# fp8 rounding in single pieces between key tiles, K and Q of the first layer evicted by ScalarE, and constants loaded in two lots

## The chip, the cores and the metric

The kernel runs on one core of a Trainium2 chip. The metric is the device time of one execution in microseconds; a time given for the kernel is the median of several runs. Profiled executions give, beside their own time, every instruction with its engine, start and duration. The engines are TensorE (PE for its matmuls, PEld for its weight loads), VectorE (DVE), ScalarE (ACT), GpSimd (POOL) and SyncE (SP), which issues most of the DMA transfers.

## What is computed

Two layers over a sequence of 4096 tokens of 256 features, in float32. Cut to what matters here:

```python
xn = layernorm(x)
# layer 0: strided sparse attention (16 heads of 16) and an fp8 product, both added to x
q, k, v = split(xn @ c_attn_w + c_attn_b)      # keys: every 8th position of all, and the own block of 128
x_q = (bf16(xn) / s_in).astype(float8_e4m3fn)
k_q = (kernel / s_k).astype(float8_e4m3fn)
y   = bf16(x_q @ k_q * (s_in * s_k)) + bias
x   = x + attention(q, k, v) @ c_proj_w + c_proj_b + y
# layer 1: rotary causal attention, a second causal attention with normalised heads, and four experts
x   = x + attention1(layernorm(x)) + experts(...)
```

The kernel does not use an fp8 type for the rounding. It rounds in float32 arithmetic: the quotient by the scale with its correction (four operations), the rounding to the spacing of fp8 by adding and subtracting a large power of two times the exponent (two on VectorE and two on GpSimd), and what lies beyond the range of fp8 (four).

## The kernel before

The sequence is worked in eight chunks of 512 positions (`NCH`, `CW`), four tiles of 128 each, and the heads in four groups of four. A *unit* is one attention kind `a` (0: sparse, 1 and 2: the causal ones), one group and one chunk of queries. A unit of the sparse attention is 1.25 key chunks long: four key tiles of strided keys and one of the own blocks. For every key tile TensorE makes scores (`st_a`), ScalarE their exponentials (`pt_a`), and TensorE multiplies them by the values (`po_a`). The maxima of a unit that comes two key chunks later are made beside this: TensorE makes products into a ring of three PSUM banks (`pms_a` strided, `pml_a` own, `pm_a` causal) and VectorE reduces them to `mx_a`. A unit ends with ScalarE's copy of `po_a` to `oc_a`.

**The order of work** is written out by hand. `Schedule` (from line 67) takes pieces with a key, and hands them out in order of the keys. One unit of the key is one key chunk of attention; key 0 is the first score tile, and what prepares the first two chunks' worth of keys has negative keys. The five engines are wrapped in `InOrder` (line 39), which makes each engine issue in just the order in which the pieces were handed out. So whatever an engine waits for, everything of its own that was handed out later waits too. As every instruction goes through the wrapper, almost all of them have line 53 in the profile, and they are told apart by their tiles.

Scores and maxima of a key tile have keys at 0.06 and 0.185 (and every quarter further), values at 0.2. `spread(start, end, todo)` places side work between key tiles: item `i` of `n` gets the key

```python
key = start + (end - start) * i / len(todo)
put(0.25 * np.floor((key - 0.2) / 0.25) + 0.212 + 1e-4 * i, *item, delay=0.9e-4)
```

so it is moved back to the slot ahead of a key tile, and all items of one slot are handed out one after the other. `block` places lists side by side in one short stretch, without this rounding to slots; chunks 4 to 7 are prepared in blocks beside the experts of an earlier chunk.

**Preparation of a chunk** (`prepare0`): `fetch` loads x and weight columns (tags `x`, `w0`); `normalised` makes the layernorm, statistics on VectorE (`bn`, `mv`, `ve`), the power and the scaling on GpSimd (`rs`, `x`); `turn` transposes on TensorE and ScalarE copies to `xt` (tag `xt0`; `ht` for the strided positions). Then K and Q products (`pk`, `pq`): VectorE evicts them with the bias (`sk`, `sq`, tag `r2`), ScalarE makes the rounded high part and GpSimd the remainder (`hl_k`, `hl_q`), and SP stores both to DRAM. V products go the same way to `v_d`. The chunk's `rounds` are, for each of the two halves of the features, a bf16 copy of `xt` by ScalarE (`xb`) and the three pieces of `quantise` (tiles `qz_x`, and `qa_x` and `qb_x` of tag `r2`, two buffers). The result `xq` goes into the products `ys` (`py`, `y`, stored to `y_d`), which need the rounded fp8 kernel `kq`; `kernel_pieces` loads that (`kern`, into the buffer `xb`) and rounds it by the same function (`qz_k`, `qa_k`, `qb_k`).

`prepare0(NCH)` is the preparation of the strided positions, K and V only. The first chunk's and the strided positions' preparation are handed out ahead of everything. `ys` of chunk 0 carries the first load of six expert weights (`weights.fetch`), after its two products.

**The constants** are loaded by ScalarE's DMA queue, one instruction each, before ScalarE's first copy.

Of the kernel before, what the change touches and what calls it, by code (L numbers as in the profile page):

```python
# [9 lines left out]
F32 = mybir.dt.float32  # L10
# [10 lines left out]
E = 256  # L21
# [88 lines left out]
def tile_two_layers(ctx: ExitStack, tc, d, out):  # L110
# [52 lines left out]
    with ExitStack() as at:  # L163
# [35 lines left out]
        for i in range(2):  # L199
# [6 lines left out]
        nc.vector.tensor_scalar(qkw[:, 0:1], qkw[:, 0:1], 0.25, None, ALU.mult)  # L206
        bqk = load("bqk", [P, 4], F32, c1)
        nc.vector.tensor_scalar(bqk[:, 0:2], bqk[:, 0:2], 0.25, None, ALU.mult)
        bv = load("bv", [P, E], F32, c1, d["bv"].partition_broadcast(P))
        bproj = load("bproj", [P, E], F32, c1, d["bproj"].partition_broadcast(P))  # L210
        fbias = load("fbias", [P, E], BF16, c1, d["fbias"].partition_broadcast(P))
        wp = [
            load(n, [P, 2, w], F32, c1, d[n].rearrange("(c p) n -> p c n", p=P))
            for n, w in (("wp0", E), ("wp1", E), ("wp2", EO))
        ]
        nw2 = load("nw2", [P, 2], F32, c1)
        gatew = load("gate", [P, 2, 4], F32, c1, d["gate"].rearrange("(c p) n -> p c n", p=P))
        tri = load("tri", [P, 2, 16], F32, c1, d["tri"].partition_broadcast(P))
        vst, vst_no = [], [0]
        for i in range(2):  # L220
            t = c1.tile([P, 2, H, D + 1], F32, name=f"vst{i}")
# [18 lines left out]
        nc.vector.tensor_tensor(sprod, scales[:, 0:1], scales[:, 1:2], ALU.mult)  # L240
        kq = c1.tile([P, 2, E], BF16, name="kq")

        def quantise(todo, q, v, k, name):


            sc = slice(k, k + 1)
            s = {}

            def quotient():
                zt = work.tile([P, CW], BF16, tag="qz", name=f"qz_{name}")  # L250
                a, b = (work.tile([P, CW], F32, tag="r2", name=f"{i}_{name}", bufs=2) for i in ("qa", "qb"))
                s.update(a=a, b=b)
                v_ = v()
                dve.tensor_scalar(zt, v_, rscale[:, sc], None, ALU.mult)
                dve.scalar_tensor_tensor(a, zt, nshi[:, sc], v_, ALU.mult, ALU.add)
                dve.scalar_tensor_tensor(b, zt, nslo[:, sc], a, ALU.mult, ALU.add)
                dve.scalar_tensor_tensor(a, b, rscale[:, sc], zt, ALU.mult, ALU.add)

            def rounded():

                a, b = s["a"], s["b"]
                dve.tensor_scalar(b.bitcast(I32), a.bitcast(I32), 0x7F800000, None, ALU.bitwise_and)
                dve.tensor_scalar(b, b, 2.0**-6, 1.5 * 2.0**20, ALU.max, ALU.mult)
                pool.tensor_tensor(a, a, b, ALU.add)
                pool.tensor_tensor(a, a, b, ALU.subtract)

            def bounded():

                a, b = s["a"], s["b"]
                dve.tensor_scalar(b.bitcast(I32), a.bitcast(I32), 0x7FFFFFFF, None, ALU.bitwise_and)  # L270
                dve.tensor_scalar(b, b, 448.0, 3e38, ALU.is_gt, ALU.mult)
                dve.tensor_scalar(b, b, 3e38, None, ALU.mult)
                dve.scalar_tensor_tensor(q(), b, 0.0, a, ALU.mult, ALU.add)

            todo += [(f, None, None) for f in (quotient, rounded, bounded)]

        def turn(todo, src, evict, name):

# [57 lines left out]
            split(s, hl)  # L336
            stored(dst, hl, half, col, what)

        def normalised(todo, x, nm):

            s = {}

            def moments():
                st = small.tile([P, TPC, 6], F32, tag="bn", name="bn" + nm)
                s["mv"] = small.tile([P, TPC, 2], F32, tag="mv", name="mv" + nm)
                for t in range(TPC):
                    dve.bn_stats(st[:, t, :], x()[:, t, :])
                    dve.bn_aggr(s["mv"][:, t, :], st[:, t, :])
                ve = small.tile([P, TPC], F32, tag="ve", name="ve" + nm)
                dve.tensor_scalar(ve, s["mv"][:, :, 1], LN_EPS, None, ALU.add)  # L350
                s["rs"] = small.tile([P, TPC], F32, tag="rs", name="rs" + nm)
                pool.tensor_tensor(s["rs"], ve, mhalf[:, :TPC], ALU.pow)

            def applied():
                for t in range(TPC):
                    pool.tensor_scalar(
                        x()[:, t, :], x()[:, t, :], s["mv"][:, t, 0:1], s["rs"][:, t : t + 1],
                        ALU.subtract, ALU.mult,
                    )

            todo += [(moments, None, None), (applied, None, None)]
# [50 lines left out]
        def prepare0(ch, w=None):  # L412
# [16 lines left out]
                w.fetch(2)  # L429

            act_piece(fetches, fetch)
            normalised(head, lambda: s["x"], nm)

            def kept(f, pt):
                if f == 0:
                    s["xt"] = work.tile([P, 2, CW], F32, tag="ht" if strided else "xt0", name="xt" + nm)
                act.copy(s["xt"][:, f, :], pt)

            turn(turns, lambda: s["x"], kept, "pt" + nm)
# [1 line left out]
            def rounded(f):  # L441
                def rounded16():
                    if f == 0:
                        s["xq"] = work.tile([P, 2, CW], BF16, tag="xq", name="xq" + nm)
                    s["xb"] = work.tile([P, CW], BF16, tag="xb", name=f"xb{f}{nm}")
                    act.copy(s["xb"], s["xt"][:, f, :])

                act_piece(rounds, rounded16)
                quantise(rounds, lambda: s["xq"][:, f, :], lambda: s["xb"], 0, f"x{f}{nm}")

            for i, (what, dst) in enumerate((("k", k_d[0]), ("q", q_d[0]))):
                if strided and what == "q":
                    continue
                for half in range(2):
                    z = {}

                    def fill(z=z, i=i, half=half, what=what):
                        feature_product(z, w[i], s["xt"], half, f"p{what}{half}{nm}")

                    def drain(z=z, half=half, what=what):  # L460
                        z["s"] = work.tile([P, CW], F32, tag="r2", name=f"s{what}{half}{nm}", bufs=2)
                        if what == "q":
                            dve.tensor_scalar(z["s"], z["p"], 0.25, bqk[:, half : half + 1], ALU.mult, ALU.add)
                        else:
                            dve.tensor_scalar(z["s"], z["p"], bqk[:, 2 + half : 3 + half], None, ALU.add)

                    def store(z=z, half=half, what=what, dst=dst):
                        split_stored(z["s"], dst, half, col, what, f"{what}{half}{nm}")

                    todo = halves_[i if own else half]  # L470
                    todo.append((fill, "bank", drain))
                    act_piece(todo, store)
# [813 lines left out]
        def kernel_pieces():  # L1286
            todo, s = [], {}

            def fetch():
                s["k"] = work.tile([P, CW], BF16, tag="xb", name="kern")  # L1290
                sp.dma_start(
                    s["k"].rearrange("p (c n) -> p c n", c=2), d["fkernel"].rearrange("(c p) n -> p c n", p=P)
                )

            todo.append((fetch, None, None))
            quantise(todo, lambda: kq.rearrange("p c n -> p (c n)"), lambda: s["k"], 1, "k")
            return todo

        place, plan = [0.0], []
# [27 lines left out]
        def spread(start, end, todo):  # L1327

            for i, item in enumerate(todo):
                key = start + (end - start) * i / len(todo)  # L1330
                put(0.25 * np.floor((key - 0.2) / 0.25) + 0.212 + 1e-4 * i, *item, delay=0.9e-4)

        w = Columns("ew", Stream.AHEAD, [("w0", 1), ("w0", 0), ("w0", 2)], "first")
        fetches, head, turns, (first, second), vs = prepare0(NCH, w)
        fetches0, head0, turns0, (first0, second0), vs0, rounds, ys = prepare0(0, w)
        block(-2000.0, (fetches + fetches0 + head + head0 + turns + turns0 + first + first0, 0.0, 1.0))
        block(-1.72, (vs + vs0 + second + second0, 0.0, 1.0), size=0.8)
        spread(0.0, 0.6, rounds)
# [197 lines left out]
```

## Time and profile before

| | us |
|---|---|
| median of 3 runs | 5078.9 (5078.31 to 5078.94) |
| the profiled execution | 5070.28 |
| its span, first to last instruction | 5068.5 |

| engine | busy us | share of the span | instructions |
|---|---|---|---|
| PE | 4862.3 | 96% | 34528 |
| PEld | 2548.9 | 50% | 34528 |
| DVE | 3711.4 | 73% | 8425 |
| ACT | 3274.0 | 65% | 6927 |
| POOL | 664.3 | 13% | 781 |

Times within the execution are counted from the start of the span. The page cuts the span into 40 equal slices and gives each engine's busy share in tenths; PEclk is the clock that the chip granted TensorE in the slice, in tenths of the full one. A view of stretches gives the same for any stretch in us. In a timeline a row is an instruction or several alike: start, duration, engine, operation, what it writes and reads, and in brackets how long its engine was idle before and what ended that. Matmul ends are modelled, so a busy PE is not PE at its peak.

### The profile page before, as it was taken

To read this page: it belongs to the slowest core of one execution; us is meant where nothing else is said; L and a number is where in the kernel's file an instruction comes from. 1 tells how busy PE (TensorE), PEld (TensorE's weight loads), DVE (VectorE), ACT (ScalarE), POOL (GpSimd) and SP (SyncE) were. 2 spreads that over 40 slices of the span, in tenths; PEclk is the share of its full clock that TensorE was granted. 3 is DMA by queue.
4 is the path that set the end of the run, shared out by engine and by line. 5 is a ranking of instruction groups with operands and counts; after the bars stand their busy time and mean duration, and the time that the engine had idled before them with its cause. 6 is when DMAs were issued, how large, how long until landed. Compare 5 with 4: busy or idle time off the path is not lost. (4 is left out here: it accounts for less than half of the span.)

```text
span 5068.5 us, 94907 instructions
## 1 busy us (share of the span) xinstructions
PE 4862.3 (96%) x34528; PEld 2548.9 (50%) x34528; DVE 3711.4 (73%) x8425; ACT 3274.0 (65%) x6927; POOL 664.3 (13%) x781
## 2 busy tenths in 40 slices
PE   6788799999999999999999999999999999999999
PEld 3445455555655564545545455544445544444445
DVE  5666685787588848897588885798984898989701
ACT  2456484676467747776477774677774777777752
POOL 3233313112100130102201002001002000000000
PEclk8889899999999999999999999999999999999999
DMA  5555545544534463434634334434333433333222
GB/s 195 179 171 187 191 162 180 179 157 157 190 134 148 141 207 128 143 130 143 202 121 152 124 126 137 164 112 145 121 126 118 161 121 128 115 108 131 94 79 75
DMA packets 480300, 732.85 MB, mean 145 GB/s; under 512 B 84053, under 2 KB 185941, under 8 KB 479833
## 3 DMA queue, kind: packets, MB, share of 16 engines
q1 hardware_dynamic: 475424, 724.33, 42.8%
q8 instruction: 273, 4.47, 0.4%
q10 hardware_dynamic: 4408, 2.46, 0.2%
q14 instruction: 195, 1.59, 0.1%
HBM read 582.71 MB, written 143.95 MB: 143 GB/s over the span
## 5 line engine op out<-in xcount | busy, mean ns | idle before, releaser
L53 ACT ACTIVATE pt_a<-st_a 128x512 f32<-128x512 f32 (+3 forms) x5248 | 2595.7, 571 | 935.1 <-PE st_a L53 862.1
L53 DVE TENSOR_REDUCE mx_a<-pm_a 128x1 f32<-128x512 f32 x3584 | 2220.8, 681 | 281.8 <-PE pm_a L53 170.8
L53 PE MATMUL pm_a<-km_a,q_a 64*128 64x512 f32 (+3 forms) x4608 | 1825.1, 435 | 59.4 <-DVE mx_a L53 49.4
L53 PE MATMUL st_a<-q_a,ke_a 64*128 64x512 f32 (+3 forms) x5632 | 1792.9, 403 | 19.8 <-ACT pt_a L53 15.6
L53 PE MATMUL st_a<-rows,pick_r 64*128 64x512 f32 (+3 forms) x5248 | 1766.6, 402 | 0.0
L53 PEld LDWEIGHTS st_a<-q_a,ke_a 64*128 64x128 f32 x5632 | 913.5, 188 | 1036.8 <-ACT pt_a L53 888.0
L53 PE MATMUL po_a<-pt_a,v 128*32 128x512 f32 (+3 forms) x11264 | 1334.6, 552 | 0.0
L53 PEld LDWEIGHTS pm_a<-km_a,q_a 64*128 64x128 f32 x4608 | 846.6, 186 | 437.8 <-DVE mx_a L53 381.7
L53 PEld LDWEIGHTS st_a<-rows,pick_r 64*128 64x128 f32 x5248 | 953.5, 187 | 61.0 <-issue 2.0
L53 DVE CUSTOM_DVE_ANT_0 pm_a<-pm_a,never_sb 128x512 f32<-128x512 f32 (+3 forms) x1024 | 479.0, 514 | 125.6 <-PE st_a L53 68.2
L53 DVE CUSTOM_DVE_ANT_0 pms_a<-pms_a,hidden_sb 128x512 f32<-128x512 f32 x512 | 339.1, 718 | 59.5 <-PE pms_a L53 46.7
L53 PEld LDWEIGHTS po_a<-pt_a,v 128*32 128x32 f32 x11264 | 228.7, 108 | 304.9 <-issue 266.8
L53 POOL CAST pad<-nm_a 128x16 fp32r<-128x16 f32 x96 | 19.6, 205 | 2280.0 <-DVE nm_a L53 2280.0
L53 PE MATMUL pms_a<-km_a,q_a 64*128 64x512 f32 x512 | 227.3, 508 | 77.8 <-DVE mx_a L53 61.3
L53 ACT CAST rows<-tu_a 8x128 fp32r<-8x128 f32 x768 | 227.1, 296 | 106.5 <-DVE tu_a L53 94.0
L53 DVE SCALAR_TENSOR_TENSOR acc_m<-pe_m,g_wt_m,acc_m 128x192 f32<-128x192 f32 x128 | 53.2, 417 | 314.7 <-PE pe_m L53 309.9
L53 PE MATMUL st_a<-mcol_sb,identb_sb 64*128 64x128 bf16 x2048 | 253.7, 225 | 0.0
L53 DVE DVE_READ_ACCUMULATOR2_ANT mx_a<- 128x1 f32 x1536 | 215.9, 141 | 0.0
L53 PEld LDWEIGHTS pms_a<-km_a,q_a 64*128 64x128 f32 x512 | 98.0, 196 | 114.5 <-DVE mx_a L53 95.5
L53 POOL TENSOR_TENSOR om_a<-od_a,rd_a 128x256 f32<-128x256 f32 x96 | 59.8, 622 | 625.6 <-DVE rd_a L53 619.9
L53 PEld LDWEIGHTS <-identb_sb 64*128 64x128 bf16 x2048 | 116.1, 97 | 13.1 <-issue 4.9
L53 DVE TENSOR_REDUCE mx_a<-pml_a 128x4 f32<-128x512 f32 x128 | 83.0, 687 | 21.1 <-PE pml_a L53 20.6
(405 smaller groups left out, 3971.4 us busy)
## 6 DMA issues: line engine op xcount, KB each, us to landing
km_a<-k_d SPq DMA_DIRECT2D x352, 512.0 KB, 4.8
ke_a<-k_d SPq DMA_DIRECT2D x352, 512.0 KB, 3.7
k_d<-hl_k SPq DMA_DIRECT2D x100, 512.0 KB, 3.5
q_d<-hl_q SPq DMA_DIRECT2D x96, 512.0 KB, 4.7
q_a<-q_d SPq DMA_DIRECT2D x96, 512.0 KB, 5.1
v<-v_d SPq DMA_DIRECT2D x352, 136.0 KB, 4.6
w_l<-in_l_dram SPq DMA_DIRECT2D x80, 256.0 KB, 2.9
w<-in_w_dram SPq DMA_DIRECT2D x69, 256.0 KB, 5.3
```

Of the source, the lines that this page charges most:

```text
L53: got = emit(*args, **kw)
```

## The change

1. `quantise` hands out its work as eleven pieces, ten with one VectorE instruction each and one with GpSimd's two, where it was three pieces of four, four and four. It takes the tag of its two float32 buffers as an argument: `r0` for chunks 0 and 1 and for the kernel, `r2` as before for the others.
2. The pieces are placed elsewhere: the kernel's at keys 0.8 to 2.0 (were 2.2 to 2.5), chunk 0's rounding at 2.0 to 4.2 (0.0 to 0.6), its products at 4.3 (2.6), chunk 1's rounding at 4.5 to 6.7 (3.0 to 3.7), its products at 6.8 (4.6), chunk 2's rounding at 7.0 to 10.0 (5.9 to 6.9), its products at 10.1 (7.2). Chunk 3's keep their place.
3. Items of one slot are ordered by a running number over all lists, where it was the number within the list.
4. Chunk 1's transposed x uses the buffer `xt`, where it was `xt0` as for the others.
5. ScalarE evicts K and Q of the first layer with one activation (factor and bias), where it was VectorE.
6. The layernorm's scaling is VectorE's for the strided positions and chunk 0, where it was GpSimd's; other chunks stay.
7. Nine constant loads (`bv`, `bproj`, `fbias`, `tri`, `gate`, three `wp`, `nw2`) are issued by SP, handed out right after the load of chunk 0's x, where ScalarE issued them among the other constants.

```diff
-        bv = load("bv", [P, E], F32, c1, d["bv"].partition_broadcast(P))
...
-        tri = load("tri", [P, 2, 16], F32, c1, d["tri"].partition_broadcast(P))
+        def fetch_constants():
+            for t, name in ((bv, "bv"), (bproj, "bproj"), (fbias, "fbias"), (tri, "tri")):
+                sp.dma_start(t, d[name].partition_broadcast(P))
+            for t, name in ((gatew, "gate"), (wp[0], "wp0"), (wp[1], "wp1"), (wp[2], "wp2")):
+                sp.dma_start(t, d[name].rearrange("(c p) n -> p c n", p=P))
+            sp.dma_start(nw2, d["nw2"])
...
-        def quantise(todo, q, v, k, name):
+        def quantise(todo, q, v, k, name, tag="r2"):
...
-            todo += [(f, None, None) for f in (quotient, rounded, bounded)]
+            def rounded():
+                pool.tensor_tensor(s["a"], s["a"], s["b"], ALU.add)
+                pool.tensor_tensor(s["a"], s["a"], s["b"], ALU.subtract)
+
+            todo += [
+                (f, None, None)
+                for f in (
+                    begun,
+                    lambda: dve.scalar_tensor_tensor(s["a"], s["z"], nshi[:, sc], v(), ALU.mult, ALU.add),
+                    lambda: dve.scalar_tensor_tensor(s["b"], s["z"], nslo[:, sc], s["a"], ALU.mult, ALU.add),
+                    lambda: dve.scalar_tensor_tensor(s["a"], s["b"], rscale[:, sc], s["z"], ALU.mult, ALU.add),
...
+                    lambda: dve.tensor_scalar(s["b"], s["b"], 2.0**-6, 1.5 * 2.0**20, ALU.max, ALU.mult),
+                    rounded,
...
+                    lambda: dve.scalar_tensor_tensor(q(), s["b"], 0.0, s["a"], ALU.mult, ALU.add),
+                )
+            ]
...
-                    pool.tensor_scalar(
+                    (eng or pool).tensor_scalar(
...
-            normalised(head, lambda: s["x"], nm)
+            normalised(head, lambda: s["x"], nm, dve if ch in (0, NCH) else None)
...
-                    s["xt"] = work.tile([P, 2, CW], F32, tag="ht" if strided else "xt0", name="xt" + nm)
+                    s["xt"] = work.tile([P, 2, CW], F32, tag="ht" if strided else "xt" if ch == 1 else "xt0", name="xt" + nm)
...
-                quantise(rounds, lambda: s["xq"][:, f, :], lambda: s["xb"], 0, f"x{f}{nm}")
+                quantise(
+                    rounds, lambda: s["xq"][:, f, :], lambda: s["xb"], 0, f"x{f}{nm}", "r0" if ch < 2 else "r2"
+                )
...
-                        if what == "q":
-                            dve.tensor_scalar(z["s"], z["p"], 0.25, bqk[:, half : half + 1], ALU.mult, ALU.add)
-                        else:
-                            dve.tensor_scalar(z["s"], z["p"], bqk[:, 2 + half : 3 + half], None, ALU.add)
+                        scale, col = (0.25, half) if what == "q" else (1.0, 2 + half)
+                        act.activation(z["s"], z["p"], AF.Identity, bias=bqk[:, col : col + 1], scale=scale)
...
-                put(0.25 * np.floor((key - 0.2) / 0.25) + 0.212 + 1e-4 * i, *item, delay=0.9e-4)
+                order[0] += 1
+                put(0.25 * np.floor((key - 0.2) / 0.25) + 0.212 + 1e-5 * order[0], *item, delay=0.9e-5)
...
+        act_piece(fetches0, fetch_constants)
...
-        spread(0.0, 0.6, rounds)
...
-        spread(2.2, 2.5, kernel_pieces())
-        spread(2.6, 2.9, ys)
-        spread(3.0, 3.7, rounds1)
+        spread(0.8, 2.0, kernel_pieces())
+        spread(2.0, 4.2, rounds)
+        spread(4.3, 4.5, ys)
+        spread(4.5, 6.7, rounds1)
+        spread(6.8, 7.0, ys1)
...
-        spread(4.6, 4.8, ys1)
-        spread(5.9, 6.9, rounds2)
-        spread(7.2, 7.4, ys2)
+        spread(7.0, 10.0, rounds2)
+        spread(10.1, 10.3, ys2)
```

More of the change, by code (lines that the diff above doesn't have):

```diff
@@ L208, in tile_two_layers @@
         nc.vector.tensor_scalar(bqk[:, 0:2], bqk[:, 0:2], 0.25, None, ALU.mult)
-        bv = load("bv", [P, E], F32, c1, d["bv"].partition_broadcast(P))
[L210 to L217, printed above, removed]
-        tri = load("tri", [P, 2, 16], F32, c1, d["tri"].partition_broadcast(P))
+        bv, bproj, fbias, nw2, gatew, tri = (
+            c1.tile(shape, dtype, name=name + "_sb")
+            for name, shape, dtype in (
+                ("bv", [P, E], F32), ("bproj", [P, E], F32), ("fbias", [P, E], BF16), ("nw2", [P, 2], F32),
+                ("gate", [P, 2, 4], F32), ("tri", [P, 2, 16], F32),
+            )
+        )
+        wp = [c1.tile([P, 2, w], F32, name=f"wp{i}_sb") for i, w in enumerate((E, E, EO))]
+        def fetch_constants():
[4 more added lines that the diff above has]
+            sp.dma_start(nw2, d["nw2"])
         vst, vst_no = [], [0]
@@ L241, in tile_two_layers @@
         kq = c1.tile([P, 2, E], BF16, name="kq")
-        def quantise(todo, q, v, k, name):
+        def quantise(todo, q, v, k, name, tag="r2"):
             sc = slice(k, k + 1)
             s = {}
[L249 to L257, printed above, removed]
-            def rounded():
[L261 to L273, printed above, removed]
-            todo += [(f, None, None) for f in (quotient, rounded, bounded)]
@@ new lines, in begun @@
+            def begun():
+                s["z"] = work.tile([P, CW], BF16, tag="qz", name=f"qz_{name}")
+                s["a"], s["b"] = (
+                    work.tile([P, CW], F32, tag=tag, name=f"{i}_{name}", bufs=2) for i in ("qa", "qb")
+                )
+                dve.tensor_scalar(s["z"], v(), rscale[:, sc], None, ALU.mult)
+            def rounded():
+                pool.tensor_tensor(s["a"], s["a"], s["b"], ALU.add)
+                pool.tensor_tensor(s["a"], s["a"], s["b"], ALU.subtract)
@@ new lines, in quantise @@
+            todo += [
[5 more added lines that the diff above has]
+                    lambda: dve.scalar_tensor_tensor(s["a"], s["b"], rscale[:, sc], s["z"], ALU.mult, ALU.add),
+                    lambda: dve.tensor_scalar(
+                        s["b"].bitcast(I32), s["a"].bitcast(I32), 0x7F800000, None, ALU.bitwise_and
+                    ),
+                    lambda: dve.tensor_scalar(s["b"], s["b"], 2.0**-6, 1.5 * 2.0**20, ALU.max, ALU.mult),
+                    rounded,
+                    lambda: dve.tensor_scalar(
+                        s["b"].bitcast(I32), s["a"].bitcast(I32), 0x7FFFFFFF, None, ALU.bitwise_and
+                    ),
+                    lambda: dve.tensor_scalar(s["b"], s["b"], 448.0, 3e38, ALU.is_gt, ALU.mult),
+                    lambda: dve.tensor_scalar(s["b"], s["b"], 3e38, None, ALU.mult),
+                    lambda: dve.scalar_tensor_tensor(q(), s["b"], 0.0, s["a"], ALU.mult, ALU.add),
+                )
+            ]
@@ L337, in split_stored, with normalised @@
             stored(dst, hl, half, col, what)
-        def normalised(todo, x, nm):
+        def normalised(todo, x, nm, eng=None):
             s = {}
@@ L448, in rounded @@
                 act_piece(rounds, rounded16)
-                quantise(rounds, lambda: s["xq"][:, f, :], lambda: s["xb"], 0, f"x{f}{nm}")
+                quantise(
+                    rounds, lambda: s["xq"][:, f, :], lambda: s["xb"], 0, f"x{f}{nm}", "r0" if ch < 2 else "r2"
+                )
             for i, (what, dst) in enumerate((("k", k_d[0]), ("q", q_d[0]))):
@@ L1295, in kernel_pieces @@
             todo.append((fetch, None, None))
-            quantise(todo, lambda: kq.rearrange("p c n -> p (c n)"), lambda: s["k"], 1, "k")
+            quantise(todo, lambda: kq.rearrange("p c n -> p (c n)"), lambda: s["k"], 1, "k", "r0")
             return todo
@@ L1330, in spread @@
                 key = start + (end - start) * i / len(todo)
-                put(0.25 * np.floor((key - 0.2) / 0.25) + 0.212 + 1e-4 * i, *item, delay=0.9e-4)
+                order[0] += 1
+                put(0.25 * np.floor((key - 0.2) / 0.25) + 0.212 + 1e-5 * order[0], *item, delay=0.9e-5)
+        order = [0]
         w = Columns("ew", Stream.AHEAD, [("w0", 1), ("w0", 0), ("w0", 2)], "first")
```

## The prediction

> **What bounds the kernel now.** I read the page's forty slices first, then the busy time of each engine per stretch, then the timeline inside the worst stretches.
>
> ```profile
> PE   6788799999999999999999999999999999999999
> PEclk8889899999999999999999999999999999999999
> ```
>
> A slice is 127 us. From slice 6 on TensorE is over 90% busy at full clock and nothing in the diff matters much; the change can only earn in the first five slices, some 630 us. The end of each attention unit of the first layer is where ScalarE copies its `oc_a`. These copies cut the stretch from the first score (77.3) to the tenth key chunk (345.9) into eight units of 1.25 key chunks with the same maxima and exponentials:
>
> ```profile
> 77.30:119.00 41.70, 29.75 (x202) 17.30 (x203) 33.16 (x83) 18.24 (x38) 15.26 (x13) 0.78 0.40 138
> 119.00:159.80 40.80, 26.83 (x197) 15.41 (x198) 21.25 (x54) 16.39 (x34) 9.88 (x12) 0.83 0.52 161
> 159.80:201.50 41.70, 24.28 (x181) 13.74 (x180) 28.14 (x74) 16.60 (x34) 14.86 (x13) 0.71 0.51 165
> 201.50:228.70 27.20, 25.91 (x194) 13.87 (x195) 17.56 (x47) 16.36 (x34) 6.98 (x8) 1.00 0.55 189
> 228.70:253.20 24.50, 20.92 (x185) 13.22 (x185) 19.84 (x53) 16.27 (x34) 7.54 (x10) 1.00 0.85 271
> 253.20:293.60 40.40, 27.36 (x201) 16.52 (x202) 25.94 (x64) 18.95 (x44) 20.71 (x19) 0.79 0.46 154
> 293.60:322.10 28.50, 25.85 (x186) 13.49 (x187) 19.08 (x54) 17.06 (x35) 12.72 (x11) 0.94 0.49 162
> 322.10:345.90 23.80, 21.97 (x182) 13.37 (x181) 17.38 (x46) 16.97 (x35) 6.07 (x7) 0.93 0.67 205
> ```
>
> Columns: stretch, its length, busy us of PE, weight load, DVE, ACT, POOL, then granted clock. Four units take 24 to 28 us, four take 40 to 42 and ran at a clock of 0.71 to 0.83. No engine fills these four: something stops them. The timeline shows what:
>
> ```profile
> 137.86 0.42 SPq L53 DMA_DIRECT2D kern<-in_fkernel_dram  x1
> 143.67 0.35 DVE L53 TENSOR_SCALAR qz_k<-kern,rscale 128x512 bf16<-128x512 bf16 x1 [6.57 <-DMA kern<-in_fkernel_dram]
> 150.16 0.43 DVE L53 TENSOR_SCALAR qb_k<-qa_k 128x512 int32<-128x512 int32 x1 [2.71 <-POOL qa_k L53]
> 151.54 0.69 DVE L53 SCALAR_TENSOR_TENSOR kq<-qb_k,qa_k 128x512 bf16<-128x512 f32 x1
> ```
>
> DVE works in order. It waits 6.57 us for the fp8 kernel, then 2.71 us for POOL's two rounding adds, with maxima queued behind; TensorE has no free bank of the ring of three and stands 13.6 us (139.3 to 153.0). The same happens with the first chunk's rounding (pauses of 4.6 us at 81.2 and 5.3 at 90.1), the second chunk's (12.0 at 165.6, 3.6 at 182.6, 1.9 at 192.5) and the third's (1.4, 1.5 and 3.2 between 245 and 267). In the 12.0 a load takes part:
>
> ```profile
> 158.57 0.33 SPq L53 DMA_DIRECT2D y_d<-y  x1
> 166.59 0.68 SPq L53 DMA_DIRECT2D x<-in_x_dram  x1
> DVE bn L53 <- DMA x<-in_x_dram: 19.7, 4, 6.2
> ```
>
> SP stood 20.2 us for the first y store, and six expert weights follow it; so the third chunk's x is issued at 166.6, and DVE waits up to 6.2 us for it with its layernorm statistics. All these pauses together are 47 us. The start has its own limit:
>
> ```profile
> 8.75 4.84 POOL L53 TENSOR_SCALAR x<-x,mv,rs 128x256 f32<-128x256 f32 x4
> 20.71 1.28 ACT L53 ACT_TABLE_LOAD   x1 [20.71 <-DMA nw_sb<-in_nw_dram]
> 22.00 2.05 ACT L53 COPY xt<-pt 128x512 f32<-128x512 f32 x4
> ```
>
> ScalarE issues constants until 20.7 and only then copies the transposed x, which was ready at 15.
>
> **The change, part by part.** *Start.* Nine constant loads leave ScalarE's queue (bv 0.44, bproj 0.46, fbias 0.34, three wp 1.50, nw2 0.48, gate 0.45, tri 0.48: 4.15 us of issue), so its first copy can come near 17 instead of 22. The layernorm of the strided and first chunk goes from POOL (4.84 and 5.12 us for four) to DVE; no row has this form there, the nearest is a 128x512 product at 0.43, so at most 1.7 for four. First x is ready at about 11, second at 18 instead of 22.5. I take -4.5 us, bounds -6 and +1 (the nine loads now compete with the x load, though they are issued behind it). SP issues them in about 4.2 us near 7 to 12; its next work was at 27.9, so that is covered.
>
> *The kernel's rounding* moves from key 2.2 to 0.8..2.0, with twelve pieces over five key tiles. SP was idle from 97.9 to 110.4, where it now falls, so the load runs ahead of its use.
>
> *The rounding of chunks 0, 1, 2* goes from keys 0..0.6, 3.0..3.7, 5.9..6.9 to 2.0..4.2, 4.5..6.7, 7..10: by the formula of `spread` two or three instructions per quarter key, never the whole. DVE's first step after POOL's adds falls, by that formula, a key tile after the step that starts them, so the 2.7 us wait for POOL has a tile of maxima as cover; if POOL is late, 2.7 us per pass come back. The other buffers (`r0`, before free until key 7.2) take the rounding out of the pair that K and Q evictions use, so neither queues for the other; the second chunk's xt in `xt` is needed because xt0 is now held to key 3. *The y stores and six weights* move from key 2.6 to 4.2, so they no longer stand ahead of the third chunk's x at key 3; behind them are then loads with over half a key (10 us) to spare. *Chunk 3* keeps 22.0..23.0: all three products in one slot and the wait for POOL inside the next, as now; nothing. *Chunks 4 to 7* are rounded beside the experts with PE near 99% busy; nothing.
>
> *Evictions.* 34 of K and Q go from DVE (751 ns) to ScalarE; nearest row there, a 128x512 eviction with a per-partition factor, 689 ns. In units of 24 to 28 us ScalarE is busy 16 to 17, so it has room; DVE loses 0.75 each and its waits for pk and pq (17.0 and 13.2 us up to 700) go to ScalarE. Queued behind such a wait are exponentials of the next tile, whose scores stand behind the same product on PE, so little is lost.
> The Trainium skill, "ScalarE: Activation LUTs", Rules for kernel authors, speaks against this part: it puts additions and products on VectorE. By it the part would cost; by these rows it is 0.06 us shorter per eviction and unloads the fuller engine.
>
> *Sum for the eight units.* The four undisturbed ones average 26.0. Three of the long ones should come to about 26.5 (they carry the same work); the fourth (253 to 294) keeps an 8.9 us pause at 277 that belongs to layer 1's layernorm, so 34. 113.5 against 164.6: -51 us, which holds the pauses and their half-clock tails. Back comes the DVE work, now in other units: six passes 37.0 us and the kernel's 5.7 (rows of 60 to 400), less eight evictions, 6.0: 36.7 us. What of it shows? Unit 228.7 to 253.2 already holds one pass of about 6 us in three lumps, and PE paused 1.44 and 1.54 for it: about half. Half of 36.7 is 18, of which 3 is in that unit already: +15. So -36 us; bounds -55 (all hidden) and -12 (nothing hidden and long units at 28).
>
> Total -4.5 - 36 = -40.5. The profiled execution took 5070.3 (span 5068.5 and 1.8 around it), 8.6 below the median of 5078.9; it would come to 5029.8, the median to 5038.4.
>
> **A rule on the clock.**
>
> ```profile
> 303.60:307.00 3.40, 1.72 (x14) 0.56 (x14) 3.37 (x10) 2.24 (x7) 3.05 (x2) 1.00 0.21 67
> 307.00:310.40 3.40, 3.21 (x16) 1.67 (x18) 3.09 (x11) 3.30 (x9) 0.43 (x1) 0.50 0.03 5
> 248.90:252.30 3.40, 1.86 (x22) 1.18 (x23) 3.30 (x10) 1.61 (x4) 0.00 (x0) 1.00 0.70 257
> 252.30:255.70 3.40, 3.40 (x48) 2.69 (x41) 3.32 (x8) 1.14 (x2) 0.00 (x0) 1.00 0.02 5
> ```
>
> PE busy 1.72 of 3.40 us (longest pause 1.7) was followed by half clock; 1.86 of 3.40 was not. So many short pauses can halve the clock too. Pauses of 1 to 1.5 us per 5 us tile, as I expect, leave a share of 0.6 to 0.7, above that line.
> The Trainium skill, "TensorE: Matmul & The Clock Gate", Part 1, gives the same window of 3413 ns, but halves the clock only after an idle window; by it nothing I expect could halve it. The row at 303.6 disagrees, which leaves the next rival alive.
>
> **Rivals.** (1) *Half clock throughout.* Rounding now sits in some 35 key tiles instead of a dozen. If it pushes PE's share under about 0.52 in most windows between key 0.8 and 10, units run at half clock: 21 us of PE work becomes 42 per unit. Four such units and four at 29 are 284, less 4.5: +11, slower. For it: 603 to 631, where lumps of rounding kept the clock at 0.58. Against: 228.7 to 253.2 held a pass at 1.00. Chance 0.05.
> (2) *Identity isn't in the table that Exp uses*: 34 evictions by two table loads of 1.283 us are 87 us of ScalarE, half of it shown: about +40. Chance 0.02. The same page of the skill on ScalarE, Table sets, has identity in every set; no run here shows it.
> (3) *DVE-bound.* Every rounding step shows in full and POOL is late: units at 30 to 33, -12 or less in all, the start's gain lost: 5068 to 5078. For it: DVE is busy 20 of 24.5 where a pass sits. Chance 0.12, most of it within 0.2%.
> (4) *All is hidden*, and the third unit falls under 25 without its x wait: -55 and -5, 5019. For it: DVE idles 5 to 10 us in each good unit. Chance 0.18.
> (5) My forecast, 5025 to 5060: 0.63.
>
> A measurement of this kernel tells 0.2% (10 us) from no change. Faster takes (4), (5) and a fifth of (3): 0.83; same 0.10; slower 0.07. The range 5012 to 5068 leaves out (1), (2), and the ends of (3) and (4).
>
> **What would show it.** Right: no PE pause over 4 us between 77 and 260; the eight units at 24 to 31 us (the sixth 34) and a clock near 1; first ScalarE copy near 17; x of the third chunk issued before DVE wants it. Wrong: granted clock under 0.8 in units 2 to 8 with pauses of 1.5 us each tile; DVE waiting 2 to 3 us for `qa_x` from POOL in most passes; more than 25 table loads; or units of 24 to 28 still at 40 for another reason.

## The result and the profile after

The changed kernel takes 5040.5 us (median of four runs, 5035.7 to 5045.6), the kernel before 5078.6 (four runs, 5070.9 to 5078.9). The ratio on record is 0.9935, with the interval 0.9923 to 0.9947; that of the two medians alone is 0.9925. So the gain is 33 to 38 us, small and clear of no change. The forecast was 5038. The profiled execution took 5038.0, against 5070.3 before, so the trace has 32.3 us to account for, where the medians have 38: single executions of one kernel spread over some 10 us.

The page of the changed kernel, its span, the slices and the busy times:

```profile
span 5036.1 us, 94879 instructions
...
PE 4853.8 (96%) x34528; PEld 2547.3 (51%) x34528; DVE 3677.4 (73%) x8399; ACT 3298.8 (66%) x6961; POOL 653.5 (13%) x773
...
PE   6888899999999999999999999999999999999999
...
PEclk8999899999999999999999999999999999999999
```

PE gained a tenth in slices 2 and 5, its clock one in 2 and 3; the rest of the span is as it was. The eight units of 1.25 key chunks after the first score are now (view of stretches, columns as before):

```profile
79.40:110.30 30.90, 26.97 (x202) 15.14 (x202) 25.05 (x66) 19.03 (x38) 9.29 (x9) 0.93 0.55 188
110.30:144.50 34.20, 27.41 (x194) 15.83 (x196) 19.63 (x52) 17.77 (x37) 11.67 (x13) 0.90 0.68 211
144.50:169.40 24.90, 20.84 (x177) 12.06 (x175) 22.94 (x66) 15.32 (x32) 10.21 (x11) 0.86 0.49 160
169.40:199.70 30.30, 27.10 (x194) 14.13 (x196) 19.16 (x53) 19.69 (x40) 10.02 (x10) 0.94 0.60 205
199.70:222.60 22.90, 21.41 (x185) 13.18 (x183) 19.80 (x55) 15.67 (x33) 9.80 (x12) 1.00 0.98 303
222.60:259.90 37.30, 25.97 (x201) 16.40 (x202) 21.22 (x62) 19.43 (x44) 15.73 (x16) 0.86 0.52 170
259.90:288.20 28.30, 25.07 (x186) 12.99 (x188) 22.31 (x60) 17.61 (x37) 15.40 (x13) 1.00 0.48 156
288.20:314.00 25.80, 21.24 (x186) 12.96 (x185) 21.80 (x53) 17.68 (x37) 10.20 (x11) 1.00 0.70 201
```

Their sum fell from 268.7 to 234.5. The whole difference of the profiled pair, cut at the first score, the end of the eighth and of the 27th unit: start +2.1 (77.3 to 79.4), eight units -34.2, units 9 to 27 +0.9 (437.6 to 438.5), the rest -1.2 (4284.9 to 4283.7): -32.4. So the units gave nearly what was forecast (-36), and the start, which was to give 4.5, cost 2. The start of the changed kernel, in its timeline:

```profile
8.89 3.27 ACTq L194 DMA_DIRECT2D first<-in_ones_dram  x2
13.00 0.29 DVE L186 CAST pick_r<-pick_f 128x256 fp32r<-128x256 f32 x1 [5.61 <-DMA pick_f<-in_pick_dram]
13.21 0.41 DVE L53 TENSOR_SCALAR x<-x,mv,rs 128x256 f32<-128x256 f32 x1
17.06 0.29 DVE L186 CAST pick_r<-pick_f 128x256 fp32r<-128x256 f32 x1 [1.52 <-DMA pick_f<-in_pick_dram]
18.00 0.15 DVE L206 TENSOR_SCALAR qkw_sb<-qkw_sb 128x1 f32<-128x1 f32 x1 [0.64 <-DMA qkw_sb<-in_qkw_dram]
18.07 0.42 DVE L53 BATCH_NORM_STATS2 bn<-x 128x6 f32<-128x256 f32 x1
18.93 1.28 ACT L53 ACT_TABLE_LOAD   x1 [18.93 <-DMA scales<-in_s_in_dram]
20.22 1.07 ACT L53 COPY xt<-pt 128x512 f32<-128x512 f32 x2
```

VectorE, which now also scales the layernorm, stands 5.61 us at a small cast of a constant (`pick_f`) that is ahead of the scaling in its order, and the statistics of chunk 0, at 10.53 before, come at 18.07, behind a second cast and a constant's multiplication. ScalarE's list of constants ends at 18.9 (20.7 before), and its first copy comes at 20.22 (22.0 before).

### The profile page after: what moved, and what is told of

Its sections match the earlier page's. It is cut to its first block, busy times and chain, and to the rows that moved or that the text cites. A ratio compares the mean times of both kernels' runs of the same rounds, so it can differ in the third digit from the quotient of the medians.

```text
span 5036.1 us, 94879 instructions
## 1 busy us (share of the span) xinstructions
PE 4853.8 (96%) x34528; PEld 2547.3 (51%) x34528; DVE 3677.4 (73%) x8399; ACT 3298.8 (66%) x6961; POOL 653.5 (13%) x773
## 5 line engine op out<-in xcount | busy, mean ns | idle before, releaser
L53 POOL CAST pad<-nm_a 128x16 fp32r<-128x16 f32 x96 | 20.3, 211 | 2266.7 <-DVE nm_a L53 2266.5
```

The source lines that it names most:

```text
L53: got = emit(*args, **kw)
```

## Experiments

Three questions were to be settled. Which part gave the units' gain: the rounding, as the prediction had it, or the engine of the evictions? Was it the single operations or their places? And what cost the start: the scaling, now on VectorE behind casts (the theory), or the nine constants on SP (the rival)?

Ratios below are to the kernel before, run beside each kernel. One caution on sizes: five of the kernels below (e1, e2, e7, e9, e10) have the eight units exactly as the changed kernel has them and gave sums of 232.7 to 238.5 for them. Differences inside these 6 us say nothing. For the first score the changed kernel has 79.4, and e5 and e6, with the same start, 79.2 and 78.3: 1 us says nothing there.

**e1, e2: the two halves of the start, each undone.** e1 gives the scaling back to GpSimd:

```diff
-            normalised(head, lambda: s["x"], nm, dve if ch in (0, NCH) else None)
+            normalised(head, lambda: s["x"], nm)
```

> The changed kernel with the layernorm's scaling of the strided positions and chunk 0 back on GpSimd; nothing else differs. Theory (VectorE's in-order stream held the start: the scaling sits behind the cast of pick_f, which waits for its load until 13.0): the strided scaling starts near 8.7 again, chunk 0's statistics near 10.5 instead of 18.1, and the first score comes 3 to 5 us sooner than the 79.4 of the changed kernel, with the eight units unchanged at 235 in sum; time 2 to 5 us under the changed kernel. Rival (the nine constants on SP compete with the loads that the start needs): the first score stays at 79 or comes later still, since GpSimd is the slower engine for the scaling; time equal or 3 us over.

e2 gives the nine constants back to ScalarE:

```diff
-        act_piece(fetches0, fetch_constants)
+        bv = load("bv", [P, E], F32, c1, d["bv"].partition_broadcast(P))     # and the other eight likewise
```

> The changed kernel with the nine constants back on ScalarE's queue. Theory (VectorE's order holds the start): VectorE still waits for pick_f, ScalarE's first copy moves from 20.2 to 22 or later, the first score stays at 79 to 82, time equal to 3 us over the changed kernel. Rival (competition of the constants on SP): pick_f lands sooner, the first score falls to 77 or under, time 2 us or more under.

First score: 78.0 and 78.1 against 79.4; ratios 0.9929 [0.9914, 0.9943] and 0.9939 [0.9924, 0.9954]. Each undoing recovers about 1.3 us, hardly more than chance, and neither gives the 3 to 5 that a single cause would. Both halves of the theory were too simple; e7 and e9 to e11 go on from here.

**e3, e4: the evictions apart from the rounding.** e3 evicts K and Q on VectorE again and leaves all else changed; e4 undoes evictions, scaling and constants together, which leaves the rounding alone.

```diff
-                        scale, col = (0.25, half) if what == "q" else (1.0, 2 + half)
-                        act.activation(z["s"], z["p"], AF.Identity, bias=bqk[:, col : col + 1], scale=scale)
+                        if what == "q":
+                            dve.tensor_scalar(z["s"], z["p"], 0.25, bqk[:, half : half + 1], ALU.mult, ALU.add)
+                        else:
+                            dve.tensor_scalar(z["s"], z["p"], bqk[:, 2 + half : 3 + half], None, ALU.add)
```

> The changed kernel with K and Q of the first layer evicted by VectorE again. Theory (the gain of the eight units is the rounding's): their sum rises by 3 to 8 us from 234.7, eight evictions of 0.75 and some waits for pk and pq; time 3 to 8 us over the changed kernel. Rival (the evictions were the gain): the sum is back over 255, time 20 us over or more.

> The kernel before with the rounding part alone: single pieces, new places, other buffers, running order, chunk 1's xt; evictions, layernorm scaling and constants as before. Theory: first score at 77.3 as before, eight units 238 to 243 in sum against 268.7, time 26 to 32 us under the kernel before. Rival (rounding gains only together with the evictions): units over 255, time within 14 us of before.

e3: 5060.2 us, 0.9970 [0.9960, 0.9979], units 245.3, units 9 to 27 443.9. e4: 5050.1, 0.9952 [0.9937, 0.9967], units 245.3. The rounding alone thus gives 23.4 of the 34.2 us (268.7 to 245.3), the evictions the other 10.8; the expectations had put 3 to 8 on the evictions. In the whole kernel e3's ratio makes them worth 0.0035, some 18 us; e4 speaks for less. It evicts on VectorE too, has 439.5 in units 9 to 27 where e3 has 443.9 and the changed kernel 438.5, and its ratio, with 2.2 us for its sooner start, gives some 11.

The 10.8 us lie in the first two units alone. These are 75.7 us long in e3 and in e4, and 65.0 to 68.0 in the six kernels that evict on ScalarE at the new places; units 3 to 8 are 169.6 in both, inside the 167.3 to 171.7 of the six. The two units in e4, to set beside the first two rows of the changed kernel above:

```profile
77.20:112.30 35.10, 28.89 (x202) 17.43 (x203) 25.87 (x68) 18.14 (x37) 9.37 (x9) 0.84 0.53 182
112.30:152.90 40.60, 30.73 (x194) 16.67 (x196) 22.71 (x55) 16.38 (x35) 11.22 (x13) 0.83 0.58 177
```

The waits of VectorE in e3 between 80 and 326 us, as total, times and longest:

```profile
DVE sq L53 <- PE pq L53: 11.9, 4, 3.9
...
DVE sk L53 <- PE pk L53: 8.4, 4, 3.8
```

In the changed kernel VectorE has neither; ScalarE has them, between 79 and 314:

```profile
ACT sq L53 <- PE pq L53: 10.9, 4, 4.1
...
ACT sk L53 <- PE pk L53: 4.6, 4, 1.5
```

So 15.5 us of waiting were not removed but moved to an engine where it costs little. On VectorE such waits hold up maxima, and with them the ring of banks that TensorE writes: TensorE waited for maxima for 35.9 us of the eight units in e3, 38.9 in e4 and 33.1 in the changed kernel, and its granted clock over them was 0.89, 0.91 and 0.93. That the place of the wait, and not the 0.75 us of work per eviction, is what pays fits the size (eight evictions are 6 us of work, the gain is 10.8), but no run separated the two. And a wait on VectorE does not always cost: of e3's, 12.5 us lie in the first two units, which are longer, and 7.3 in the fourth, which is not (32.1 in e3 and 30.7 in e4, against 30.2 to 31.5). Why the latter are free stays open.

**e5, e6: single operations or places.** e5 keeps the changed places, but hands the rounding out in the three lumps of before; e6 keeps the single operations, at the places of before.

```diff
# e5
-            todo += [(f, None, None) for f in (begun, ...)]        # eleven pieces
+            todo += [(f, None, None) for f in (quotient, rounded, bounded)]
# e6
-        spread(0.8, 2.0, kernel_pieces())
-        spread(2.0, 4.2, rounds)
...
+        spread(0.0, 0.6, rounds)
+        spread(2.2, 2.5, kernel_pieces())
...
```

> The changed kernel with the rounding handed out in three pieces of four, two and GpSimd's two, and four again, as before; places, buffers and all else as changed. Theory (the places carry the gain: each lump now has its own slot, the load of x and of the fp8 kernel come ahead of their use, and GpSimd's adds have a tile of maxima as cover): eight units 237 to 246 in sum against 234.5, time 2 to 10 us over the changed kernel. Rival (the single operations carry it): units 255 or more, time 20 us over.

> The changed kernel with the single operations at the keys of before (rounding 0 to 0.6, 3.0 to 3.7, 5.9 to 6.9, the fp8 kernel 2.2 to 2.5, products and the six weights at 2.6 to 2.9). Theory (places): a slot again holds eight or more operations, the third unit waits for x behind the y stores again, the fp8 kernel is used right after its load: units 250 to 262 in sum, time 15 to 28 us over the changed kernel. Rival (single operations): units 240 or less, time within 6 us of the changed kernel.

e5: 5039.4, 0.9933 [0.9919, 0.9948], units 236.1: the changed kernel's time. e6: 5085.3, 1.0020 [1.0010, 1.0029], units 273.3: the whole gain is gone, although evictions and constants stay changed. By the ratios that is some 43 us over the changed kernel, where 15 to 28 were expected. So at the old places neither single operations nor the evictions gained anything. The other buffers (`r0`, `xt`) and the running order of a slot are in e4, e5 and e6 alike, and no run tested them by themselves. The first four units of e6:

```profile
78.30:124.70 46.40, 29.96 (x202) 17.46 (x203) 31.29 (x81) 19.45 (x40) 15.01 (x13) 0.78 0.32 113
124.70:163.60 38.90, 26.31 (x198) 15.23 (x198) 19.88 (x53) 17.85 (x36) 9.89 (x12) 0.82 0.54 167
163.60:204.70 41.10, 24.50 (x181) 14.21 (x179) 28.12 (x74) 16.80 (x34) 14.76 (x13) 0.75 0.51 168
204.70:232.00 27.30, 25.80 (x194) 13.84 (x195) 15.23 (x43) 18.96 (x38) 6.98 (x8) 1.00 0.60 198
```

and of e5:

```profile
79.20:113.40 34.20, 29.64 (x202) 17.00 (x203) 25.53 (x66) 19.26 (x39) 11.27 (x11) 0.86 0.48 167
113.40:139.00 25.60, 24.45 (x194) 14.65 (x196) 19.49 (x52) 17.71 (x37) 9.04 (x12) 1.00 0.85 271
139.00:164.90 25.90, 20.04 (x177) 11.58 (x176) 23.94 (x66) 15.30 (x33) 10.67 (x11) 0.93 0.49 165
164.90:191.20 26.30, 25.29 (x194) 13.75 (x196) 19.37 (x51) 19.54 (x39) 10.07 (x10) 1.00 0.62 223
```

Eleven pieces in a stretch of 0.3 to 1 key fall several to a slot and are handed out in one go, lumps under another name: 46.4, 38.9 and 41.1 us again. Lumps over the longer stretches do as well as single operations in sum, but the sum hides two differences: the first two units are shorter with lumps (59.8 us against 65.0 to 68.0), above all the second, 25.6 against 34.2, and units 3 to 8 longer (176.3 against 167.3 to 171.7). So the splitting gains some 5 to 9 us behind the second unit. What it loses in the second the changed kernel's timeline shows, rows of GpSimd and of VectorE:

```profile
113.76 1.27 POOL L53 TENSOR_TENSOR hl_q<-sq,hl_q 128x512 fp32r<-128x512 f32 x1 [6.00 <-issue]
114.99 2.60 POOL L53 TENSOR_TENSOR qa_k<-qa_k,qb_k 128x512 f32<-128x512 f32 x2
117.62 0.43 DVE L53 TENSOR_SCALAR qb_k<-qa_k 128x512 int32<-128x512 int32 x1 [6.97 <-POOL qa_k L53]
```

GpSimd's two adds for the kernel stand behind the remainder of Q, which waits for ScalarE's eviction of Q (at 112.29) and its rounded part (at 113.01). VectorE's next step waits 6.97 us for them, and TensorE stands from 114.19 to 118.70. The adds could have begun at 108.04, when VectorE's step ahead of them was done; GpSimd had nothing to do from 107.77 to 113.76 but wait. By the formula of `spread` the adds (item 7 of 12 between keys 0.8 and 2.0, key 1.5) fall a slot behind that step (item 6, key 1.4), into the slot of VectorE's next one (item 8, key 1.6), and GpSimd's order has Q's remainder ahead of them. In e5, with four items, the adds have key 1.4, one slot sooner. There GpSimd runs them at 111.16, ahead of Q's remainder at 116.74, and VectorE does not wait.

**e7, e8: the start mended, and the remaining waits.** e7 gives the loads of `pick` and the ones buffers of their own and hands the casts out after the first chunk's products. e8 adds to it three empty pieces after GpSimd's adds for the kernel, three after each bf16 copy, and layer 1's layernorm scaling of chunks 0 and 1 on VectorE.

```diff
# e7
-            pick_f = work.tile([P, 2, P], F32, tag="xt", name=f"pick_f{i}")
...
-            nc.vector.tensor_copy(pick[:, i], pick_f)
+        pick_f = [work.tile([P, 2, P], F32, tag="pt", name=f"pick_f{i}", bufs=12) for i in range(3)]
...
+        act_piece(first0, cast_constants)          # the five casts, and the ones likewise
# e8, besides
+                for _ in range(3):
+                    act_piece(rounds, lambda: None)
...
+            todo[8:8] = 3 * [(lambda: None, None, None)]
...
-            normalised(todo, lambda: s["x"], nm)
+            normalised(todo, lambda: s["x"], nm, dve if ch < 2 else None)
```

> The changed kernel with the start loosened: the three loads of pick_f and the two of ones get buffers of their own (of the tag pt), so that none waits for a cast, and their casts are handed out on VectorE after the first products. Layernorm scaling stays on VectorE, the nine constants on SP. Theory (the chain of pick_f loads and casts held both ScalarE's queue and VectorE): ScalarE's first copy near 15 to 17 instead of 20.2, chunk 0's statistics near 10.5, first score 71 to 75 instead of 79.4, units unchanged; time 4 to 8 us under the changed kernel. Rival (the loads themselves are late, for want of DMA bandwidth or issue slots): first score 78 or later, no change in time.

> The kernel of the loosened start, with three more edits for the pauses that are left: three empty pieces after the bf16 copy of a rounding pass and three after GpSimd's adds of the fp8 kernel, so that VectorE's next step falls at least a slot later, and layer 1's layernorm scaling of chunks 0 and 1 on VectorE. Theory: VectorE's waits for xb (10.2 us) and for the fp8 kernel's adds (7.0) mostly go, the 9.1 us pause in the sixth unit falls to about 5; units 222 to 230 in sum; time 8 to 20 us under the changed kernel. Rival (these waits are covered, another takes their place): units 232 to 236, time that of the loosened start.

e7: 5039.2, 0.9931 [0.9916, 0.9946]; first score at 78.7, so the expectation failed. Its timeline, rows of VectorE and of ScalarE's queue:

```profile
8.82 3.83 ACTq L185 DMA_DIRECT2D pick_f<-in_pick_dram  x3
...
17.73 0.15 DVE L209 TENSOR_SCALAR qkw_sb<-qkw_sb 128x1 f32<-128x1 f32 x1 [6.56 <-DMA qkw_sb<-in_qkw_dram]
```

The scaling now starts at 9.15, but VectorE then stands 6.56 us at the next constant, `qkw`, still ahead of chunk 0's statistics; and ScalarE's three issues take 3.83 us.

e8: 5033.2, 0.9920 [0.9905, 0.9934], units 228.2, 10.3 below e7's 238.5 and 4.5 below the lowest sum of the kernels with unchanged units. The second unit fell from 34.2 to 25.6, the sixth from 37.4 to 35.2; the fifth rose from 23.9 to 26.9. The fall of the second unit is the work of the adds. As item 7 of 15 they have key 1.36, a slot sooner than in the changed kernel, and GpSimd has them ahead of Q's remainder:

```profile
106.86 2.62 POOL L53 TENSOR_TENSOR qa_k<-qa_k,qb_k 128x512 f32<-128x512 f32 x2 [0.36 <-DVE qb_k L53]
112.44 1.28 POOL L53 TENSOR_TENSOR hl_q<-sq,hl_q 128x512 fp32r<-128x512 f32 x1 [2.96 <-ACT hl_q L53]
```

The first two units took 56.3 us (65.0 to 68.0 in the kernels of unchanged units), units 3 to 8 171.9 (167.3 to 171.7), no shorter. VectorE's four waits for the bf16 copy, 10.2 us, are gone, but four for GpSimd's adds of x (`qa_x`), 10.6 us, stand in their place: in two of these passes the empty pieces put VectorE's step ahead of the adds and its step behind them into one slot, and in the other two GpSimd does other work first (until 256.5 and 291.2). So the late adds for the kernel were a real cost, and what the waits for the bf16 copy cost stays open.

**e9, e10, e11: the two causes of the start.** e9 is the changed kernel with the nine constants issued by SP much later (key -1.74). e10 is e7 with the arithmetic on constants (`qkw`, `bqk`, the scales) handed out after the transposes of chunk 0. e11 has both and the edits of e8.

```diff
# e9
-        act_piece(fetches0, fetch_constants)
+        put(-1.74, fetch_constants)
# e10
-        nc.vector.tensor_scalar(qkw[:, 0:1], qkw[:, 0:1], 0.25, None, ALU.mult)
...
+        act_piece(turns0, scale_constants)         # the same seven operations
```

> The changed kernel with the second lot of nine constants handed out only after the first loads of q and k (key -1.74), so that SP issues nothing but x and weights in the first 30 us. Theory (ScalarE's and SP's issues go at one common pace of about 0.45 us each between 8 and 19 us, so a load moved from one to the other buys nothing, and one moved out of the stretch does): ScalarE's list ends 3 to 4 us sooner, first copy 16 to 18 instead of 20.2, first score 76 to 78 instead of 79.4; VectorE's wait for pick_f stays. Rival (only VectorE's order counts): first score 79 or later.

> The kernel of the loosened start (e7_start), with the arithmetic on the loaded constants (qkw, bqk, scales) handed out on VectorE after the transposes, so that chunk 0's statistics stand behind no load but their own. Theory (both the order on VectorE and the issue pace count): statistics near 11 instead of 17.8, chunk 0's x ready near 16 instead of 23.3; ScalarE's list still ends near 19, so its four copies run at 20.5 to 23 and the first score comes near 76 instead of 78.7. Rival (issue pace alone): first score within 0.7 of 78.7.

> All of it: the kernel e8_all with VectorE's constant arithmetic handed out after the transposes and the second lot of constants after the first loads of q and k. Theory: first copy near 15 to 17, all four by 19, first score 71 to 74 instead of 78.4; eight units 226 to 232 in sum; time 4 to 7 us under e8_all, 38 to 48 under the kernel before. Rival (the late lot collides with the loads of q, k and v and gives the time back before the first score): first score 77 or later.

First score: e9 77.5, e10 75.0, e11 71.0 (changed kernel 79.4). Times: 5042.2 (0.9943 [0.9928, 0.9958]), 5034.3 (0.9927 [0.9912, 0.9942]) and 5024.5 (0.9909 [0.9892, 0.9925]). The start of e11:

```profile
8.42 1.41 ACTq L185 DMA_DIRECT2D pick_f<-in_pick_dram  x3
...
10.70 0.41 DVE L53 BATCH_NORM_STATS2 bn<-x 128x6 f32<-128x256 f32 x1
...
15.13 1.28 ACT L53 ACT_TABLE_LOAD   x1 [15.13 <-DMA scales<-in_s_in_dram]
16.42 2.05 ACT L53 COPY xt<-pt 128x512 f32<-128x512 f32 x4
```

Both causes are real, and each hides the other. e9 brings the first copy to 18.3 and leaves VectorE's order: 1.9 us, little more than chance. e10 brings the statistics to 10.7 and leaves ScalarE's list, to 18.8: 4.4 us. Together 8.4. Without the nine issues of SP beside them the three `pick` issues take 1.41 us from the first to the last, not 3.83 as in e7, the list ends at 15.1, and the first copy comes at 16.4, where the prediction had it ("near 17"). e11 is the fastest kernel here, 0.9% under the one before, with units of 228.2.

## The prediction point by point

- **What bounds, and where the gain lies: right.** Behind unit 8 the profiled pair differs by 0.9 and -1.2 us; chunks 3 to 7 gave nothing, as stated.
- **Eight units, -36: -34.2 measured, in part by luck.** The sum was -51 for the four long units and +15 for the work that comes back in the others. The long ones gave -37.3 (164.6 to 127.3): "about 26.5" for three of them came as 30.9, 34.1 and 25.0. The four others rose by 3.2 only (104.1 to 107.3). By parts, too, two errors of opposite sign lie inside. The evictions entered the sum as 6.0 us of VectorE's work, about half of it shown, so 3; they gave 10.8 there (e3). The step that failed is "so little is lost" for the waits on `pk` and `pq`: it was read as a cost on ScalarE, and the gain on VectorE, where 20.3 us of them stood ahead of maxima in e3 (11.9 + 8.4) and 15.2 in the kernel before, was not put in. The rounding was put at the rest, some -33, and gave -23.4 (e4).
- **Third chunk's x: right.** Its load is issued at 140.6 (before 166.6), and the third unit went from 41.7 to 25.0.
- **The cover for "the 2.7 us wait for POOL": right for the six passes, wrong for the kernel.** No pass of x made VectorE wait more than 0.13 us for `qa_x`. The price "if POOL is late" was 2.7 per pass; for the kernel it came as 6.97 us of VectorE and 4.51 of TensorE. "A key tile after" holds by the formula there too (items 6 and 8); the step that failed is that POOL would start the adds as soon as VectorE's step was done. POOL, in order too, had Q's remainder ahead. Four waits on ScalarE's bf16 copy (`xb`), 10.2 us in all and 4.3 the longest, were not foreseen; first use and copy share a slot. So the units are 23 to 34 us and not 24 to 31, and a pause over 4 us remains before 222.
- **Sixth unit, 34: 37.3.** Its pause at layer 1's layernorm stayed, 9.09 us (242.41 to 251.50) where 8.9 was named.
- **Start, -4.5, bounds -6 and +1: +2.1, outside the bounds.** Two steps failed. Of the 4.15 us of issue that were to leave ScalarE only 1.8 did (table load at 20.71, then 18.93): the nine issues went on beside ScalarE's and slowed them (e9, e11). "First x is ready at about 11": VectorE's order ahead of the scaling was not read; the 1.7 us for four scalings was nearly right (2.01 in e7), but it began at 13.2 behind a cast. That the nine loads were "covered" on SP held for SP alone: the nine took 3.6 us of issue, between 7.9 and 17.5 where "near 7 to 12" was forecast.
- **The rivals.** (2) is out: 25 table loads before and after, which agrees with the Trainium skill, "ScalarE: Activation LUTs", Table sets, where identity is in every set. (3), a VectorE bound, and (4), all hidden, did not come; neither did (1): the clock of the units is 0.86 to 1.00.
- **The eviction's price, right.** 689 ns were taken; `sk` takes 0.69 us on ScalarE, 0.75 on VectorE. The Trainium skill, "ScalarE: Activation LUTs", Rules for kernel authors, puts additions and products on VectorE and gives a speed in bf16 as its reason; here, in float32, the 10.8 us of e3 and e4 speak for ScalarE.

For the profiled pair -40.5 was forecast and -32.3 came: 6.6 of the difference is the start's, 1.8 the units'. That the medians lie 2 us from the forecast is luck in part, by the executions shown: the one before was 8.6 under the median it was scaled to, the one after 2.5 under its own.

## What to carry to other kernels

Where engines work in order, ask of each moved instruction what stands ahead of it on its new engine and what stands behind it: a small cast waiting for a load cost more here than the work that was moved. The kernel's adds, behind Q's remainder on GpSimd, were the second such case. A wait is cheaper on the engine with less urgent work behind it, so moving an eviction can pay by its wait rather than by its work; here it paid in two units of eight. Spread side work over a longer stretch before splitting it finer: without the longer stretch the splitting gained nothing (e6), and with it some 5 to 9 us by units 3 to 8. Compare unit by unit: equal sums can hide a gain and a loss.

## What was not expected of the hardware

**Issues of two engines went at one pace.** In these starts an issue takes about half a microsecond on average, gaps included, whether one engine issues or two: 24 by ScalarE alone from 6.96 to 20.68 before (0.57 each), 22 by ScalarE and SP from 7.84 to 18.89 after (0.50), 24 by both from 7.10 to 18.83 in e10 (0.49), 15 by ScalarE in e11 from 7.08 to 15.10 (0.53). The same 15 took 11.7 us in e10 and 8.0 in e11. The Trainium skill, "DMA: Bandwidth & Descriptors", Issuing engines are not separate DMA queues, lets issuing from several engines save the issue time of the sequencer; by that ScalarE would have saved all of the 4.15 us. The rows show 1.8, so here it holds in part. What sets the pace is not shown.

**Half clock without an idle window.** In eight of these profiles (before, after, e1, e3, e5 to e8), from 50 to 1300 us in windows of 3.413 us (the clock changed only at multiples of that), every window at full clock with TensorE busy under half of it was followed by one at half clock, 99 of 99. Only 14 of these were idle throughout; in 34 the longest pause was at most 2 us, in 7 under 1 us. At a busy share of 0.50 to 0.59 it was 30 of 57, at 0.60 to 0.69 11 of 81, at 0.9 and over 1 of 2127. Return took a busier window: below 0.8, 124 of 124 stayed at half clock; at 0.8 to 0.9, 1 of 36 came back, at 0.9 to 1.0, 14 of 33, and of wholly busy ones 134 of 148. The share alone is no rule for the whole kernel: from 1300 to 5000 us, in the same profiles, 50 of 148 windows with a share of 0.8 to 0.9 were followed by half clock, where it was 6 of 137 before. Two windows of the changed kernel:

```profile
182.50:185.90 3.40, 0.96 (x6) 0.45 (x6) 2.12 (x6) 3.17 (x7) 1.59 (x1) 0.99 0.96 279
185.90:189.30 3.40, 3.40 (x12) 0.79 (x13) 3.11 (x8) 0.60 (x1) 0.69 (x2) 0.50 1.04 372
```

The longest pause in the first is 2.44 us. The Trainium skill, "TensorE: Matmul & The Clock Gate", Part 1, has the clock halved after an idle window in its table of the two states; these rows need none. The prediction's line, a share of about 0.52, was near.
